# A macaron block on one core: the last two diagonal steps of causal attention in one PSUM bank, with another beginning of the first MLP and three other orders

## The chip, the core and the metric

The kernel runs on one core of a Trainium2 chip. The metric is the time on the device in microseconds (us), median of the runs shown. The core has five engines with a queue each, which run side by side: TensorE (PE, matrix products, with its weight loads shown apart as PEld), VectorE (DVE), ScalarE (ACT), GpSimd (POOL) and SyncE (SP, which here only issues DMAs). Each queue is worked off in order. PE writes to PSUM, which has 8 banks of 512 floats on each of the 128 partitions; everything else lies in SBUF.

## The reference

One block of 2048 tokens with 512 features: half an MLP, causal attention with 16 heads of 32, and half of the same MLP again, each behind a layer norm without weights. The MLP's weights are 4-bit codes with a scale for each 32.

```python
def _layernorm(x, axis=-1, eps=1e-05):
    m = jnp.mean(x, axis=axis, keepdims=True)
    v = jnp.var(x, axis=axis, keepdims=True)
    return (x - m) / jnp.sqrt(v + eps)
...
    qkv = jnp.einsum('bsd,ed->bse', x, w_qkv) + b_qkv
...
    scores = jnp.einsum('bhqd,bhkd->bhqk', q, k) / math.sqrt(Hd)
    causal = jnp.triu(jnp.full((S, S), -jnp.inf, dtype=scores.dtype), k=1)
    scores = scores + causal[None, None]
    attn = jax.nn.softmax(scores, axis=-1)
    out = jnp.einsum('bhqk,bhkd->bhqd', attn, v)
...
    gate = jnp.einsum('th,nh->tn', xt, Wg)
    up = jnp.einsum('th,nh->tn', xt, Wu)
    gelu = jnp.tanh(0.7978845608028654 * (gate + 0.044715 * gate ** 3)) * gate * 0.5 + gate * 0.5
    inter = gelu * up
    out = jnp.einsum('tn,hn->th', inter, Wd)
...
x = x + 0.5 * _L0_ffn_ref(_layernorm(x, axis=-1), ...)
x = x + _L0_attn_ref(_layernorm(x, axis=-1), ...)
x = x + 0.5 * _L0_ffn_ref(_layernorm(x, axis=-1), ...)
```

## The kernel before

Everything is computed in fp32 unless said otherwise. Each engine runs its instructions in the order in which the program issues them; that order is written out by hand in the loops below, and the waits between engines follow from which tile an instruction reads or writes and when a tile's buffer comes free.

**First MLP (`ffn`, L188).** The products are done with seven-product forms of 2 x 2 blocks (Strassen-Winograd). `slot` (L346) runs one unit of it: for the gate (m = 0) and then for the up weights (m = 1), the seven products in the order 1, 2, 6, 7, 5, 4, 3, each into one PSUM bank by `product` (L339, matmuls at L341), with the additions that turn them into four results spread over ACT, DVE and POOL behind each. After each product `pump(rate)` issues `rate` background steps (dequantisation of later weights), and then one group of `groups`, a list of other work such as normalisation. The beginning (L516 to L540) loads tokens and codes on SP's queue, normalises the first two token blocks with `Norm` (`n0`, `n1`; moments, scales, four `normal` and four `transposed` steps), dequantises the first gate and up weights (`gate`, `up`: six steps each half) and forms sums of transposed tokens (`token_sums`, L312) that products 3 to 7 need.

**Attention (`attention`, L1070).** Heads go in 8 pairs; a pair works on 4 blocks g of 512 queries. The keys go in chunks c of 128. Block g needs the chunks below it, 4g of them ("whole" ones), and four on the diagonal, c = 4g to 4g + 3, whose scores have 512, 384, 256 and 128 columns. That is 40 steps a pair: 4, 8, 12, 16. `STARTS` (0, 4, 12, 24) are the steps at which the blocks begin. `order(g)` puts the diagonal last, except in block 3, where half of the whole chunks come behind it.

A step (`step`, L1389) has for each of the two heads (a = 0, 1) the score matmuls into one PSUM bank (L1403 adds the negated row maxima as three rows in bf16, L1412 the scores), a mask on the diagonal (DVE L1428 for a = 0; for a = 1 an ACT copy L1432 and a POOL select L1433), the exponentials on ACT (L1439, L1441), and then in `tail` the sums of two steps' exponentials for the denominators (`sum`, POOL and DVE, L1461 and L1463) and, two steps later (`pending`), the `values` (L1332): matmuls at L1323 with the values, and for the sums with ones, into the one accumulator bank `av` (`ps_acc`, one buffer). `denominators` pops one pair's sum in every second step and at the end of a block. The two last diagonal steps are not summed; their exponentials go to the ones matmuls directly.

After the last step of a block ACT copies the accumulator to `both` (L1345; the pool `an` has two buffers of it), and for pairs 1 to 6 the denominators are turned over DMAs and inverted (`inverse`, four steps later). `divided` (POOL L1377) multiplies numerators with inverses, four pieces a block, at the steps that `when` names: 10, 10, 11 and 11 steps later for block 3, which is in the next pair.

Pairs 0 and 7 (`DOUBLE`) run two steps at a time (`attend(p, 2)`): both score sections, then both `rest`, then both `tail`. Their sums are split between DVE (a = 0) and POOL (a = 1), and their division is done at once in `chunk` (reciprocals on DVE L1366, products on POOL L1369).

In pairs 1 to 6 each step runs together with a step of `maxima(p + 1)` (L1231): scores of a query chunk against up to 512 keys (L1248), whose row maxima DVE takes (L1260, or L1256 with the mask on the diagonal). At a block's end `finish` reduces them (`nmax`, L1266), and POOL splits them into three bf16 pieces (`split`, L1271 and L1274), five small operations; `rows` transposes them three steps later (PE L1284, ACT L1288). `maxima(0)` and `maxima(1)` run together in a loop ahead (the front loop, L1528), with `take` pieces of the projections after each step. In the other pairs projection work fills the diagonal steps (`after_step`, L1493): `fill` holds a block's pieces and the number of diagonal steps left, 4 at the start.

**Orders touched.** In pair 7 the normalisation for the second MLP (`Norm("f2", ...)`) is put behind steps of block 3 by the two tuples `after`. In the second MLP (`second_ffn`, `pair`, L724) the four down sums of a piece are put at places 2, 5, 2 and 2 of a pair's work.

Of the kernel before, what the change touches and what calls it, by code (L numbers as in the profile page):

```python
# [19 lines left out]
P = 128  # L20
# [10 lines left out]
STARTS = (0, 4, 12, 24)  # L31
# [5 lines left out]
def macaron_kernel(ctx: ExitStack, tc: tile.TileContext, x, packed, scales, wqk, bqk, wv, bv, wo, bo, out):  # L37
# [150 lines left out]
    def ffn(phase, finish, behind, loads, ready=(), first_w=None):  # L188
# [8 lines left out]
        with tc.tile_pool(name=f"w{phase}", bufs=1) as wp, tc.tile_pool(name=f"dq{phase}", bufs=1) as dq, tc.tile_pool(  # L197
# [148 lines left out]
            def slot(g, rows, tp, sums, fill, rate, groups=()):  # L346


                groups = list(groups)
                b = token_factors(tp)  # L350
                inter = [
                    ap.tile(
                        [P, 2, 512], F32, tag=f"i{rows.h}_{tb}" if rows.h == 0 else f"i1_{tb % 2}",
                        name=f"inter_{phase}_{g}_{rows.h}_{tb}",
                    )
                    for tb in (2 * tp, 2 * tp + 1)
                ]
                gate = {}

                def gelu(cell, c):  # L360
                    nc.scalar.activation(c, c, AF.Gelu_apprx_tanh)
                    gate[cell] = c

                def gated(cell, c):
                    tt(inter[cell % 10 - 1][:, cell // 10 - 1, :], gate[cell], c, ALU.mult)

                for m, done in ((0, gelu), (1, gated)):
                    a = rows.factors(m)
                    nm = f"{phase}_{g}_{rows.h}_{tp}"
                    names = ("pg", "pu")  # L370

                    def temp(k, bufs=2):
                        return ap.tile([P, 512], F32, tag=k, name=f"{k}_{m}_{nm}", bufs=bufs)

                    for i in ORDER:
                        ps = ps_one.tile([P, 512], F32, tag="one", name=f"{names[m]}{i}_{nm}")
                        product(ps, a[i], b[i])
                        if i == 1:
                            u2 = temp("u2")
                            nc.scalar.copy(u2, ps)  # L380
                        elif i == 2:
                            c11 = temp("c11")
                            tt(c11, ps, u2, ALU.add)
                            done(11, c11)
                        elif i == 6:
                            tt(u2, ps, u2, ALU.add)
                        elif i == 7:
                            u3 = temp("u3")
                            tt(u3, ps, u2, ALU.add)
                        elif i == 5:  # L390
                            u4 = temp("u4")
                            nc.scalar.copy(u4, ps)  # L392
                            c22 = temp("c22")
                            tt(c22, ps, u3, ALU.add)
                            nc.gpsimd.tensor_tensor(u4, u4, u2, ALU.add)  # L395
                            done(22, c22)
                        elif i == 4:
                            tt(u3, ps, u3, ALU.add)
                            done(21, u3)
                        else:  # L400
                            tt(u4, ps, u4, ALU.add)
                            done(12, u4)
                        pump(rate)
                        if groups:
                            run(groups.pop(0))
                        if sums:
                            sums.pop(0)()
                        if fill:
                            fill.pop(0)()
                return inter  # L410
# [105 lines left out]
            if phase == 1:  # L516
                load_x(1)
                rows.load(0)
# [4 lines left out]
                tags = ["u3", "u3", "c11", "c11"]  # L523
                n0 = Norm("f1", 0, xT[0], normed)
                n1 = Norm(
                    "f1", 1, xT[1], lambda nm: ap.tile([P, D], F32, tag=tags.pop(), name=nm, bufs=2),
                    on_act=(), on_pool=(0, 1),
                )
                gate, up = rows.steps(0), rows.steps(1)
                tiles = n0.tiles()  # L530
                run(n0.moments + [n0.scales] + n1.moments + tiles[:6] + gate[:2] + [n1.scales] + tiles[6:])
                run([n1.normal[i] for i in (0, 2, 1, 3)] + [n1.transposed[i] for i in (2, 0, 3, 1)] + gate[2:])
                run(token_sums(0) + up)
# [10 lines left out]
            early = [[]]  # L544
            for n in (n2, n3):
                early += [[n.moments[0]], [], [n.moments[1]], [], [n.scales]]
            late = staggered(n2, n3) + [[s] for s in token_sums(1)]
            fill = ([], [])
            for g in range(NG):
                if g == 0:  # L550
                    first = [slot(g, rows, 0, *fill, 2, early)]
# [94 lines left out]
    def second_ffn(finish, ready, slots):  # L646
# [9 lines left out]
        with tc.tile_pool(name="w2", bufs=1) as wp, tc.tile_pool(name="act2", bufs=1) as ap:  # L656
# [371 lines left out]
            for n in range(2 * NP + 1):  # L1028
# [21 lines left out]
                if pieces:  # L1050
                    for k, f in enumerate(down_sums):
                        if due == (1, 1, 2, 3)[k]:
                            mine[(2, 5, 2, 2)[k]].append(f)
# [16 lines left out]
    def attention(xT, xT_f, wqk_wv, next_w):  # L1070
        with tc.tile_pool(name="aw", bufs=1) as aw, tc.tile_pool(name="qk", bufs=1) as qkp, tc.tile_pool(
# [159 lines left out]
            def maxima(p):  # L1231
# [5 lines left out]
                for g in range(NB):  # L1237
                    parts = an.tile([P, 2, 4, g + 1], F32, tag=f"parts{g}", name=f"parts_{p}_{g}")
                    whole = [(i, kb) for i in range(4) for kb in range(g)]
                    steps = around(g, whole, [(i, g) for i in (3, 2, 1, 0)])  # L1240
                    for i, kb in steps:
                        n = 512 if kb < g else (i + 1) * P
                        ps = [None, None]

                        def matmuls(a):
                            r = quadrant(p, a)
                            ps[a] = ps_one.tile([P, 512], F32, tag="one", name=f"pm_{p}_{g}_{i}_{kb}_{a}")
                            nc.tensor.matmul(  # L1248
                                ps[a][:, :n], lhsT=q[r, bass.ts(4 * g + i, P)], rhs=k[r, kb * 512 : kb * 512 + n],
                                start=True, stop=True,  # L1250
                            )

                        def rest(a, now):
                            most, scores = parts[:, a, i, kb : kb + 1], ps[a][:, :n]
                            if kb == g:
                                nc.vector.tensor_tensor_reduce(  # L1256
                                    scores, scores, mask_f[:, 512 - n :], 1.0, MASKED, ALU.add, ALU.max, accum_out=most
                                )
                            else:
                                nc.vector.tensor_reduce(most, scores, AX.X, ALU.max)  # L1260
# [36 lines left out]
            def attend(p, width):  # L1297

# [4 lines left out]
                def order(g):  # L1305
                    return around(g, list(range(4 * g)), list(range(4 * g, 4 * g + 4)))

                def columns(product, operand, off, **kw):


                    for a in range(2):
                        for h in range(2):
# [4 lines left out]
                            elif off <= (2 + h) * P:  # L1317
                                dst_ = avs[0][group, product, P:]
                                rhs = operand[:, a, (2 + h) * P : (3 + h) * P]
# [10 lines left out]
                def denominators():  # L1330
                    for operand, off in summed.pop(0):
                        columns(1, operand, off)  # L1332

                def values(g, n, off, pt):
                    c = order(g)[n]
# [3 lines left out]
                    columns(0, pt, off, v=vals[:, c, p % 4, :], start=(n == 0))  # L1339
                    last = n + 1 == len(order(g))  # L1340
                    if (n > 0 and n % 2 == 0) or last:
                        denominators()
# [46 lines left out]
                def step(g, n, copied):  # L1389
                    c = order(g)[n]  # L1390
                    off = max(0, c - 4 * g) * P
                    ps = [None, None]
# [6 lines left out]
                    def maxrows(a):  # L1399
# [3 lines left out]
                        nc.tensor.matmul(  # L1403
                            ps[a][:, off:],
                            lhsT=ones_b[r.start : r.start + 3, :],
                            rhs=m[r.start : r.start + 3, at_ * 512 + off : (at_ + 1) * 512],
                            start=True, stop=False,
                        )

                    def matmuls(a):  # L1410
                        r = rows_of(a)
                        nc.tensor.matmul(  # L1412
                            ps[a][:, off:],
                            lhsT=k[r, bass.ts(c, P)],
                            rhs=q[r, g * 512 + off : (g + 1) * 512],
                            start=False, stop=True,
                        )

                    def rest():
                        pt = pp.tile([P, 2, 512], F32, tag="pt", name=f"pt_{p}_{g}_{c}")  # L1420
                        scale = 1.0 / math.sqrt(HD)
                        plain = [off, off]
                        if c >= 4 * g:


                            for a in range(2 if p in DOUBLE else 1):
                                own = ps[a][:, off : off + P]
                                nc.vector.tensor_tensor(own, own, mask_k, ALU.add)  # L1428
                            if p not in DOUBLE:
                                plain[1] = off + P  # L1430
                                own = pt[:, 1, off : off + P]
                                nc.scalar.copy(own, ps[1][:, off : off + P])  # L1432
                                nc.gpsimd.affine_select(  # L1433
                                    out=own, in_=own, compare_op=ALU.is_ge, fill=MASKED, base=0,
                                    pattern=[[1, P]], channel_multiplier=-1,
                                )
                        for a in range(2):
                            if plain[a] < 512:
                                nc.scalar.activation(pt[:, a, plain[a] :], ps[a][:, plain[a] :], AF.Exp, scale=scale)  # L1439
                        if plain[1] > off:  # L1440
                            nc.scalar.activation(own, own, AF.Exp, scale=scale)  # L1441
                        two.append((pt, off))
# [296 lines left out]
```

## Time and profile before

| | |
|---|---|
| median of 3 runs | 3132.38 us (3132.2 to 3133.98) |
| profiled execution, its own time | 3135.08 us |
| its span | 3133.2 us |
| PE busy in the span | 3096.3 us |
| pairs 1 to 6, 1370 to 1950 us | PE busy 577.60 of 580, POOL 344.05, DVE 352.96, ACT 298.86 |
| pair 7 and the way to the second MLP, 1950 to 2041 us | PE busy 88.56 of 91, granted clock 0.96 |
| first 20 us | PE busy 7.71 |
| 20 to 70 us | PE busy 46.56 of 50 |

The span runs from the first to the last recorded instruction of the profiled execution; 1.9 us of its time lie around the span. Busy times are sums over an engine's instructions in a stretch. A timeline row gives the start, the time from the first start to the last end of a group of like instructions, the engine, the line, output and inputs by name and the number of instructions; in square brackets stands the time that the engine stood idle before, and what ended it. The granted clock is TensorE's, 1.00 being full speed.

### The profile page before, as it was taken

The page shows a single profiled execution, that of the slowest core. Times are in us where ns is not written, and L with a number is a line of the kernel's source. Part 1 is how long each engine was busy: PE and PEld are TensorE (multiplying, and loading weights), DVE is VectorE, ACT ScalarE, POOL GpSimd, SP SyncE. Part 2 cuts the span into 40 slices and gives each one's busy share as a digit, 9 for nine tenths or more (in the row PEclk, how much of TensorE's full clock was granted, in tenths as well). Part 3 has the DMA queues.
Part 4 walks back from the last instruction along what each step waited for, and adds up shares of the span by engine and source line. Part 5 has one row for each costly group of instructions (what it writes and reads, how often), then busy time and mean ns, then how long its engine had stood idle before and what let it go on. Part 6 is the DMA issues. An engine that isn't in the chain of part 4 may idle for free.

```text
span 3133.2 us, 45074 instructions
## 1 busy us (share of the span) xinstructions
PE 3096.3 (99%) x16608; PEld 1995.8 (64%) x16608; DVE 2069.6 (66%) x3217; ACT 1043.0 (33%) x2029; POOL 1521.9 (49%) x1512
## 2 busy tenths in 40 slices
PE   7999999999999999999999999999999999999999
PEld 4556565656565565444335434478888888888887
DVE  7676666666666656755564566777666776666676
ACT  5111111111111123265553456443333343333332
POOL 3757575857667672365663466522232223223221
PEclk9999999999999999999999999999999999999999
DMA  4223122212122221000000000064444445344442
GB/s 141 85 83 118 69 93 88 98 61 97 61 98 79 80 93 34 5 11 9 12 9 7 29 21 11 14 193 131 125 135 128 128 130 168 116 125 128 127 128 61
DMA packets 260394, 260.66 MB, mean 83 GB/s; under 512 B 20720, under 2 KB 224592, under 8 KB 256080
## 3 DMA queue, kind: packets, MB, share of 16 engines
q1 hardware_dynamic: 260176, 257.80, 25.3%
q8 instruction: 131, 2.15, 0.3%
q14 instruction: 87, 0.71, 0.1%
HBM read 175.74 MB, written 79.89 MB: 82 GB/s over the span
## 4 chain that ended last, share of the span: by engine, by line
PE 94%; DVE 2%; ACT 1%; issue 1%; POOL 1%; DMA 0%; SPq 0%; POOLq 0%; ACTq 0%; DVEq 0%
PE po L440 12%; PE d_f L748 12%; PE pu L341 12%; PE pg L341 12%; PE av L1323 7%; PE pod_f L879 7%; PE pm L1248 6%; PE f_f L748 6%; PE pqk L1146 4%; PE pof_f L879 3%; PE e_f L748 3%; PE ps L1403 2%; PE pp L1201 2%; PE pv L1175 2%; PE ps L1412 2%; PE poe_f L879 1%
## 5 line engine op out<-in xcount | busy, mean ns | idle before, releaser
L1439 ACT ACTIVATE pt<-ps 128x512 f32<-128x512 f32 (+3 forms) x616 | 289.1, 531 | 189.8 <-PE ps L1412 113.3
L748 PE MATMUL d_f<-ys_f,ring 128*128 128x256 f32 x1216 | 319.6, 383 | 6.1 <-DVE o_f L781 5.8
L1260 DVE TENSOR_REDUCE parts<-pm 128x1 f32<-128x512 f32 x384 | 245.1, 685 | 111.7 <-PE pm L1248 111.5
L1463 POOL TENSOR_TENSOR sum<-pt,pt 128x512 f32<-128x512 f32 (+1 forms) x210 | 249.2, 1205 | 121.2 <-ACT pt L1439 99.1
L1248 PE MATMUL pm<-kT,qT 32*128 32x512 f32 (+3 forms) x1280 | 297.2, 576 | 0.3 <-ACT kT L1152 0.3
L1412 PE MATMUL ps<-qT,kT 32*128 32x512 f32 (+3 forms) x1200 | 261.2, 539 | 0.0
L748 PEld LDWEIGHTS d_f<-ys_f,ring 128*128 128x128 f32 x1216 | 226.7, 190 | 53.6 <-DVE o_f L781 21.5
L802 DVE TENSOR_TENSOR o_f<-o_f,o_f 128x1024 f32<-128x1024 f32 x128 | 203.6, 1601 | 62.6 <-ACT o_f L787 57.9
L440 PEld LDWEIGHTS po<-wd,inter 128*128 128x128 f32 x1024 | 194.4, 190 | 77.5 <-issue 56.0
L440 PE MATMUL po<-wd,inter 128*128 128x256 f32 x1024 | 241.1, 379 | 0.0
L341 PE MATMUL pg<-xT_f,w 128*128 128x512 f32 x512 | 239.2, 595 | 1.1 <-ACT u L380 1.1
L341 PE MATMUL pu<-xT_f,w 128*128 128x512 f32 x512 | 238.0, 592 | 0.0
L894 POOL TENSOR_TENSOR xq<-xq,d_f 128x512 f32<-128x512 f32 x48 | 63.7, 1328 | 311.3 <-DVE xq L888 230.7
L454 POOL TENSOR_TENSOR xq<-xq,d 128x512 f32<-128x512 f32 x124 | 161.5, 1313 | 92.4 <-DVE xq L448 56.0
L894 POOL TENSOR_TENSOR xq_second<-xq_second,d_f 128x512 f32<-128x512 f32 x45 | 60.6, 1347 | 280.5 <-DVE xq_second L888 213.3
L1323 PE MATMUL av<-pt,vals 128*32 128x256 f32 (+1 forms) x2432 | 190.8, 369 | 1.9 <-ACT both L1345 1.7
L440 PEld LDWEIGHTS po<-wd,s 128*128 128x128 f32 x768 | 145.5, 190 | 57.9 <-issue 39.9
L395 POOL TENSOR_TENSOR u<-u,u 128x512 f32<-128x512 f32 x64 | 81.9, 1279 | 205.9 <-ACT u L392 205.9
L440 PE MATMUL po<-wd,s 128*128 128x256 f32 x768 | 181.4, 379 | 0.0
L802 POOL TENSOR_TENSOR o_f<-o_f,o_f 128x1024 f32<-128x1024 f32 x44 | 119.0, 2704 | 124.2 <-ACT o_f L787 123.1
L341 PE MATMUL pg<-xsum,w 128*128 128x512 f32 x384 | 177.8, 592 | 0.0
L341 PE MATMUL pu<-xsum,w 128*128 128x512 f32 x384 | 177.7, 592 | 0.0
(231 smaller groups left out, 6358.7 us busy)
## 6 DMA issues: line engine op xcount, KB each, us to landing
wd_f<-kept SPq DMA_DIRECT2D x112, 256.0 KB
kept<-wd SPq DMA_DIRECT2D x8, 1792.0 KB
xq<-in_x SPq DMA_DIRECT2D x16, 256.0 KB
pk<-in_gate_codes SPq DMA_DIRECT2D x16, 256.0 KB
sc<-in_gate_scales SPq DMA_DIRECT2D x32, 128.0 KB
pk<-in_up_codes SPq DMA_DIRECT2D x16, 256.0 KB
sc<-in_up_scales SPq DMA_DIRECT2D x32, 128.0 KB
pk<-in_down_codes SPq DMA_DIRECT2D x16, 256.0 KB
```

What stands on the lines that cost most here:

```text
L341: nc.tensor.matmul(ps, lhsT=a[:, j, :], rhs=b[:, j, :], start=(j == 0), stop=(j == 1))
L440: nc.tensor.matmul(ps[:, j, :], lhsT=a[i][:, k, bass.ts(2 * q + j, P)], rhs=b[i][:, k, :], start=(k == 0), stop=(k == 1),)
L454: adder.tensor_tensor(dst, dst, other, ALU.add)
L748: nc.tensor.matmul(ps[:, k, :], lhsT=fa[k][y], rhs=fb[k][y], start=first and k == 0, stop=True, skip_group_check=True,)
L802: sums.append(lambda: eng.tensor_tensor(dst, dst, other, ALU.add))
L879: nc.tensor.matmul(ps[:, j, :], lhsT=a[:, k, bass.ts(2 * q + j, P)], rhs=wd[:, PLACE[i], k, :], start=new and j == k == 0, stop=True, skip ...
L1248: nc.tensor.matmul(ps[a][:, :n], lhsT=q[r, bass.ts(4 * g + i, P)], rhs=k[r, kb * 512 : kb * 512 + n], start=True, stop=True,)
L1260: nc.vector.tensor_reduce(most, scores, AX.X, ALU.max)
L1323: nc.tensor.matmul(dst_, lhsT=lhsT, rhs=rhs, start=kw.get("start", False), stop=True, skip_group_check=True)
L1412: nc.tensor.matmul(ps[a][:, off:], lhsT=k[r, bass.ts(c, P)], rhs=q[r, g * 512 + off : (g + 1) * 512], start=False, stop=True,)
L1439: nc.scalar.activation(pt[:, a, plain[a] :], ps[a][:, plain[a] :], AF.Exp, scale=scale)
L1463: eng.tensor_tensor(s[:, a, off_2:], one[:, a, off_2:], other[:, a, off_2:], ALU.add)
```

## The change

**Attention.** In pairs 1 to 6 the last two diagonal steps become one. Its scores stand in one PSUM bank: 256 columns of chunk 4g + 2 at 0, and 128 of chunk 4g + 3 at 256. A pair has 36 steps, so `STARTS` is (0, 3, 10, 21); pairs 0 and 7 keep (0, 4, 12, 24) as `STARTS_2`. The maxima do the same for query chunks 1 and 0 of a block's diagonal, so the front loop has 36 steps too, with another `take`. A block's fill is spread over 3 diagonal steps instead of 4 in pairs 1 to 6. `order(g)` now yields tuples of chunks, and `values`, `columns`, `maxrows` and `matmuls` loop over the parts of a step.

The rule for when a sum's denominators are issued has become general: each sum is kept with its block and step, and `denominators` issues those of an earlier step. The sum of two steps is made as soon as `two` holds two.

```diff
-STARTS = (0, 4, 12, 24)
+STARTS = (0, 3, 10, 21)
+STARTS_2 = (0, 4, 12, 24)
...
                 def order(g):
-                    return around(g, list(range(4 * g)), list(range(4 * g, 4 * g + 4)))
+                    last = [2, 3] if width == 2 else [(2, 3)]
+                    return around(g, [(c,) for c in range(4 * g)], [(4 * g, ), (4 * g + 1, )] + [
+                        tuple(4 * g + i for i in (t if width == 1 else (t,))) for t in last
+                    ])
...
-                def denominators():
-                    for operand, off in summed.pop(0):
-                        columns(1, operand, off)
+                def denominators(g, n, last):
+                    while summed and summed[0][0] == g and (summed[0][1] < n or last):
+                        for operand in summed.pop(0)[2]:
+                            columns(1, *operand)
...
                     last = n + 1 == len(order(g))
-                    if (n > 0 and n % 2 == 0) or last:
-                        denominators()
+                    denominators(g, n, last)
...
+                    parts = [(off, 0)] if len(cs) == 1 else [(2 * P, 2 * P), (3 * P, P)]
...
-                        two.append((pt, off))
-                        pending.append(lambda args=(g, n, off, pt): values(*args))
+                        if len(cs) == 1:
+                            two.append((pt, off))
+                        else:
+                            summed.append((g, n, [(pt, *part) for part in parts]))
+                        pending.append(lambda args=(g, n, parts, pt): values(*args))
...
-                        if n % 2 == 1:
+                        if len(two) == 2:
...
-                take = 3 if n < 3 else 4 if n == 39 else 1 if n in (10, 11, 22, 23, 32) else 2
+                take = 4 if n == 35 else 3 if n in (0, 1, 2, 9, 20, 29) else 2
...
-                        fill = [fills[STARTS.index(n)], 4]
+                        fill = [fills[starts.index(n)], 4 if p in DOUBLE else 3]
```

In the maxima, `parts_of` holds one part of a step, or two where the key block is the diagonal one and i is 1:

```diff
-                    steps = around(g, whole, [(i, g) for i in (3, 2, 1, 0)])
+                    steps = around(g, whole, [(i, g) for i in (3, 2, 1)])
...
+                        parts_of = [(i, 0, n)] + [(0, n, n + P)] * (kb == g and i == 1)
```

**The beginning of the first MLP.** The first gate codes are loaded ahead of the second four token tiles; the first gate half is dequantised before the first tiles are normalised; the second block's normalisation is done on ACT alone; the first slot runs products 1 and 2 of gate and up first, pumps nothing after its first five products and three steps after each of the others, and the transposes of the second block and the token sums come between its products. `slot` takes an `order` and a list as `rate` for that.

```diff
             if phase == 1:
+                rows.load(0)
                 load_x(1)
-                rows.load(0)
                 rows.load(1)
...
-                tags = ["u3", "u3", "c11", "c11"]
+                tags = ["u3", "u3", "u4", "u4"]
                 n0 = Norm("f1", 0, xT[0], normed)
-                n1 = Norm(
-                    "f1", 1, xT[1], lambda nm: ap.tile([P, D], F32, tag=tags.pop(), name=nm, bufs=2),
-                    on_act=(), on_pool=(0, 1),
-                )
+                n1 = Norm("f1", 1, xT[1], lambda nm: ap.tile([P, D], F32, tag=tags.pop(), name=nm, bufs=2))
...
-                run(n0.moments + [n0.scales] + n1.moments + tiles[:6] + gate[:2] + [n1.scales] + tiles[6:])
-                run([n1.normal[i] for i in (0, 2, 1, 3)] + [n1.transposed[i] for i in (2, 0, 3, 1)] + gate[2:])
-                run(token_sums(0) + up)
+                run(n0.moments + [n0.scales] + gate[:4] + tiles + gate[4:])
+                run(n1.moments + [n1.scales] + n1.normal + up)
+                sums_0 = token_sums(0)
...
-            early = [[]]
+            t = n1.transposed
+            early = [[t[0]], t[1:3], [t[3]] + sums_0, []]
...
+            first_order = [(m, i) for m in range(2) for i in ORDER[:2]] + [(m, i) for m in range(2) for i in ORDER[2:]]
...
-                    first = [slot(g, rows, 0, *fill, 2, early)]
+                    first = [slot(g, rows, 0, *fill, [0] * 5 + [3] * 9, early, first_order)]
```

**Two more orders.** Pair 7's normalisation is put behind other steps, and one down sum of the second MLP comes four places later in one pair.

```diff
-                            after = ((0, 1, 4, 5, 6, 6, 7, 8, 9, 10), (3, 9, 11, 11, 12, 12, 13, 13, 14, 15))[tb][i]
+                            after = ((0, 1, 4, 5, 8, 8, 9, 9, 10, 11), (3, 9, 11, 11, 12, 13, 13, 14, 14, 15))[tb][i]
...
-                            mine[(2, 5, 2, 2)[k]].append(f)
+                            mine[(2, 5, 6 if n == NP + 2 else 2, 2)[k]].append(f)
```

## The prediction

> **What bounds the kernel now.** I read the busy times first, then the chain of waits, then a table of stretches, to see where TensorE (PE) isn't full.
>
> ```profile
> PE 3096.3 (99%) x16608; PEld 1995.8 (64%) x16608; DVE 2069.6 (66%) x3217; ACT 1043.0 (33%) x2029; POOL 1521.9 (49%) x1512
> PE 94%; DVE 2%; ACT 1%; issue 1%; POOL 1%; DMA 0%; SPq 0%; POOLq 0%; ACTq 0%; DVEq 0%
> ...
> 1370.00:1950.00 580.00, 577.60 (x5916) 243.46 (x5914) 352.96 (x886) 298.86 (x722) 344.05 (x523) 1.00 0.05 13
> ```
>
> PE is the bound: 99% busy, 94% of the chain. In the third line (pairs 1 to 6 of the attention; after the stretch's length come busy PE, weight loads, DVE, ACT, POOL) PE rests 2.4 of 580 us. So a PE section removed is a gain, but a wait put in front of PE costs in full. POOL is only 344 busy, but its queue is in order, and the change reorders it.
>
> **Part 1: two diagonal steps in one.** A step is a section S of scores (PE L1403, L1412, L1248), perhaps a section F of projection pieces, and a section A of values (L1323). The PE timeline of pair 2, block 1, prices S by column count:
>
> ```profile
> 1479.05 0.33 PE L1403 MATMUL ps<-wo_bo,ones_b 3*128 3x384 bf16 x1
> ...
> 1479.97 0.64 PE L1323 MATMUL av<-pt,vals 128*32 128x256 f32 x8
> ...
> 1484.17 0.28 PE L1403 MATMUL ps<-wo_bo,ones_b 3*128 3x256 bf16 x1
> ...
> 1484.82 0.64 PE L1323 MATMUL av<-pt,vals 128*32 128x256 f32 x8
> ...
> 1485.83 0.22 PE L1403 MATMUL ps<-wo_bo,ones_b 3*128 3x128 bf16 x1
> ...
> 1486.27 0.64 PE L1323 MATMUL av<-pt,vals 128*32 128x128 f32 x8
> ```
>
> From S's first start to A's: 0.92 for 384 columns, 0.65 for 256, 0.44 for 128. The merged step has the columns of the last two, 384 in all: 0.65 + 0.44 - 0.92 = 0.17 saved (0.29 in pairs without fill, where the 256 section takes 0.77). The two A sections behind become one; a section's fixed part is what S leaves at no columns, 0.44 - 0.25 = 0.19, and of it I count 0.14. So 0.31 in each of 16 blocks of pairs 2 to 5, 0.43 in 8 of pairs 1 and 6: **-8.4**. Fill: one piece takes 1.06, two in a section 1.92, so two one-piece sections joined save 0.20, in 12 blocks of pairs 3 to 5: **-2.4**. Front (maxima of pairs 0 and 1): 0.65 + 0.43 - 0.85 = 0.23 and 0.20 of fill in 4 blocks: **-1.7**. Together -12.5. All of it is PE time; ACT's and POOL's fewer instructions lie beside it.
>
> **What it puts in front of PE.** In the built order POOL now has, in the merged step, the five small operations that split the maxima AHEAD of the diagonal sum (L1461, L1463), and sum_2_1 ahead of the last two `divided` of the block 3 before. `both` has two buffers: the ACT copy of block 1 waits for those last two, and the next block's values wait for the copy, since the accumulator has one bank. Rows of before, same place, POOL, then ACT and PE:
>
> ```profile
> 1485.70 0.40 POOL L1461 COPY sum<-pt 128x256 f32<-128x256 f32 x1
> 1486.07 1.96 POOL L1463 TENSOR_TENSOR sum<-pt,pt 128x384 f32<-128x384 f32 x2
> 1488.10 1.52 POOL L1377 TENSOR_TENSOR attnT<-both,den 32x256 f32<-32x256 f32 x2
> 1489.70 0.29 POOL L1433 TENSOR_SCALAR_AFFINE_SELECT pt<-pt 128x128 f32<-128x128 f32 x1
> 1489.94 0.22 POOL L1271 CAST split<-nmax 128x8 bf16<-128x8 f32 x1
> ...
> 1491.39 1.52 POOL L1377 TENSOR_TENSOR attnT<-both,den 32x256 f32<-32x256 f32 x2
> 1492.99 2.50 POOL L1463 TENSOR_TENSOR sum<-pt,pt 128x512 f32<-128x512 f32 x2
> ```
> ```profile
> 1492.94 0.59 ACT L1345 COPY both<-av 128x512 f32<-128x512 f32 x1 [0.66 <-POOL attnT L1377]
> ```
> ```profile
> 1493.58 0.64 PE L1323 MATMUL av<-pt,vals 128*32 128x256 f32 x8 [0.62 <-ACT both L1345]
> ```
>
> The wait exists already: the copy starts as the last `attnT` ends, and PE stands still for 0.62. Now the new order, from the start of the merged scores at 0. DVE starts at 0.95 (as in the 384 step: 1479.05 to 1480.00), four maxima of 0.34 and 0.21 and two masks of 0.24 end at 2.5, nmax at 2.9. POOL: splits 1.4 to 4.3; sum 0.37 + 1.95 to 6.7 (its first half 5.7); `divided` 1.52 to 8.3; sum_2_1 2.50 to 10.8; `divided` 1.52 to 12.35; ACT copy 0.59; PE resumes at 13.0. PE by itself comes there at 0.92 + 1.00 + 1.18 + 0.57 + 1.19 + 1.43 + 0.34 + 1.26 = 7.9, and the fill of the merged step (pairs 2 to 6: 0, 1.06, 3.63, 1.06, 0). Stalls 5.1, 4.1, 2.5 (pair 4: the sum waits for exponentials until 9.4 there), 4.1, 5.1 = 20.9; pair 2 and pair 6 pay 1.2 and 1.3 already: **+18.4**. Bounds +6 (POOL 2.5 earlier) and +22.
>
> The sum itself: PE wants it in the merged step's A, near 5.5, and the second half is there at 6.7. Stall 1.1 in pairs without fill there: three blocks of pair 1, blocks 0 and 2 of pairs 2 and 6 (block 1 lies in the stall above, block 3 has no splits, fill covers the rest): 7 x 1.1 = **+7.7**, bounds 0 and 11.
>
> A pause can cost more than itself. Around 2002 PE paused three times (0.51, 0.66, 0.28), and the granted clock was 0.83, 0.50, 0.50, 0.50 in the next four stretches of 2 us: some 3 us lost. Pauses of 1.1, 0.8 and 1.5 at 46, 51 and 57 left it at 1.00. For five pauses of 2.5 to 5 us I take one such loss, **+3**, between 0 and 15.
>
> [...]
>
> **Part 2: denominators of pairs 0 and 7.** These run two steps at once; the rule `summed[0][1] < n` now asks for a double step's sum in the very next A, one double earlier.
>
> ```profile
> 1344.34 2.33 POOL L1369 TENSOR_TENSOR attnT<-both,den 32x128 f32<-32x128 f32 x4
> ...
> 1346.76 1.27 POOL L1463 TENSOR_TENSOR sum<-pt,pt 128x512 f32<-128x512 f32 x1
> ```
>
> That sum lies behind four chunk products and ends at 1348.03; A began at 1345.40, and after two value groups (0.45 each) and its first half PE would want it at 1346.4: 1.65 late. So by block: pair 0 about 0.7, 1.65, 1.6; pair 7 about 0.4, 1.75, 1.0: +7.1, bounds +3 and +11 (where ACT's exponentials end later). The last diagonal pair of block 3 is now added, 8 passes instead of 16: -0.4. **+6.7**.
>
> **Part 3: the beginning.** Gate codes come before x tile 1, so the first product starts near 15.05 instead of 19.64. But the up weights are ready at 20.8 only, and token sums come after the copies of tile 1, which stand behind ACT's normalisation and its first gelu: 28.3 by DVE's rows (1.44 + 1.63 behind 25.2), against 23.6. PE idles some 3 there, ten products of 1.72 follow, and the slot ends near 45.6 against 45.1. Later pauses of 3.4 shrink with 3 us less backlog on DVE; half of that, 1.7, against the 0.5 and a chance of the 3 us clock loss: I take **0**, bounds -4 and +4. SP's loads of x tiles 2 and 3 come later, not wanted before 30.
>
> **Part 4: three orders.** Pair 7's normalisation goes behind the next scores, around the pauses at 2002: -1, bounds -4 and +1. One down sum on DVE moves four places near 2574, where PE rests 3.4 of 20 us: 0, bounds -1 and +1. **-1**.
>
> **Sum:** -12.5 + 18.4 + 7.7 + 3 + 6.7 + 0 - 1 = **+22.3**. The profiled execution took 3135.08 (span 3133.2 and 1.9 around it), so 3157.4; the median shown is 2.7 below that execution: **3155 us**. The likeliest case's own range is 3143 to 3165.
>
> **Rivals.** *Gains alone (faster).* One mechanism: POOL reaches the last `divided` before PE does. Place: block 1 of pairs 2 to 6, and with it the diagonal sums. It decides when POOL's chain from nmax is 5 us shorter than I add up. For it: the page calls POOL's spans rough, and POOL is 41% idle there. Against: the rows lie end to end, and before already waits at this place. The sums of pairs 0 and 7 go through the same queue, so 18.4, 7.7, 3 and 7.1 all fall away: -13.9, 3118 to 3119.
>
> *Only the boundary wait.* Sums and doubles hidden, since PE, once delayed, comes later to all of them: -12.5 + 18.4 - 1 = +4.9, 3137. For it: one stall absorbs the next; against: pair 1 has no boundary stall, and pairs 0 and 7 lie elsewhere.
>
> *All upper ends.* +22, +11, five clock losses 15, doubles +11, beginning +4, less 13.5: +49.5, 3182 at the most; 3173 with three losses fewer. For it: 2002; against: 46 to 57.
>
> *The merge doesn't save.* If a PSUM bank written by two groups made S cost both sections (1.09), -8.4 falls to about -3: 3160, inside the main range.
>
> **Chances.** Forecast, with the unsaved merge: 0.52; boundary alone 0.15; gains alone 0.19; upper ends 0.14. About 0.2%, 6.3 us, can be told from no change: below 3126.1 faster, above 3138.7 slower. Of gains alone 0.17 is faster and 0.02 same (parts of it); of the boundary alone 0.10 is same, 0.05 slower. Faster 0.17, same 0.12, slower 0.71. The range leaves out about a tenth at each end: 3123 to 3168.
>
> **What would show it.** After: S of the merged step 0.92; in block 1 of pairs 2 to 6 `both` on ACT with an idle time ended by POOL attnT of 2 to 5 us, and PE av idle behind it; PE av on POOL sum in the diagonal blocks and in pairs 0 and 7; the stretch of pairs 1 to 6 about 15 us longer; the first pg near 15 and a PE gap ended by token sums near 28. A `both` that doesn't wait, or a shorter stretch, makes it wrong.

## The result and the profile after

The changed kernel takes 3172.56 us (median of 4 runs, 3169.96 to 3174.82) against 3133.06 before (the three runs known and one more): ratio 1.0124, 95% interval 1.0111 to 1.0136. It is slower by 39.5 us, some 17 more than forecast, and 4.6 beyond the top of the range. The profiled execution took 3169.96 us with a span of 3167.9 (before: 3135.08 and 3133.2). Each later ratio is to runs of before made beside that run, whose medians go from 3133.06 to 3134.63 us, so what two kernels differ by can come out 1 to 2 us apart by ratios and by times. Only runs in the chip's fast state count; two of the eight with three buffers (4840 and 5301 us) and one of before beside them (18198 us) were in a slow one.

Two lines of the page (busy times, and the chain of work that ended last), and the stretch of pairs 1 to 6 in the table of stretches (its length, busy PE, weight loads, DVE, ACT, POOL, the granted clock):

```profile
PE 3107.0 (98%) x16592; PEld 2008.7 (63%) x16592; DVE 2076.0 (66%) x3218; ACT 1038.0 (33%) x1961; POOL 1516.0 (48%) x1488
PE 91%; POOL 3%; DVE 3%; ACT 1%; issue 1%; DMA 1%; SPq 0%; DVEq 0%; POOLq 0%; ACTq 0%
...
1370.00:1990.00 620.00, 595.66 (x5988) 259.28 (x5984) 361.87 (x892) 293.86 (x656) 341.36 (x500) 0.98 0.05 12
```

PE now rests 24 us in that stretch instead of 2.4, POOL and DVE have 3% each of the chain, and over the whole kernel PE's busy time went up, from 3096.3 to 3107.0, though 16 matmuls left it: the clock is 0.98 in that stretch, so the same work takes longer. Idle time and slow time are two losses, and only the first stands in a table of waits.

Where the 34.7 us of span came from can be read off ACT's copies of `both`, one at each block's end, in the two timelines. How much later (or earlier) than before a block ends after the change, in us, and what the prediction's terms gave for the same stretch:

| stretch | measured | predicted |
|---|---|---|
| to the start of the front loop (first score matmul at 1191.38, before 1196.35) | -5.0 | 0 |
| front loop, to the first copy | +1.1 | -1.7 |
| rest of pair 0 | +4.8 | +3.9 |
| pair 1 | +2.7 | +1.6 |
| pairs 2 to 6 | +31.1 | +16.7 |
| pair 7 | +1.9 | +1.7 |
| second MLP and end | -1.9 | 0 |

Most of the miss lies in pairs 2 to 6, where block 1 of each pair costs 4.4, 4.8, 3.2, 4.8 and 4.4. The small gain in the second MLP isn't explained by a run; before lost 1.7 us of clock there, at 2589 to 2592, and after none past 2063. The same place as in the prediction, pair 2, in the timelines of POOL, ACT and PE; the merged scores start at 1489.23:

```profile
1492.83 0.22 POOL L1278 CAST split<-nmax 128x8 bf16<-128x8 f32 x1 [1.48 <-DVE nmax L1273]
...
1494.10 0.40 POOL L1488 COPY sum<-pt 128x256 f32<-128x256 f32 x1
1494.46 1.95 POOL L1490 TENSOR_TENSOR sum<-pt,pt 128x384 f32<-128x384 f32 x2
1496.49 1.51 POOL L1388 TENSOR_TENSOR attnT<-both,den 32x256 f32<-32x256 f32 x2
1498.08 2.48 POOL L1490 TENSOR_TENSOR sum<-pt,pt 128x512 f32<-128x512 f32 x2
1500.64 2.30 POOL L1388 TENSOR_TENSOR attnT<-both,den 32x256 f32<-32x256 f32 x3
```
```profile
1502.19 0.59 ACT L1356 COPY both<-av 128x512 f32<-128x512 f32 x1 [4.66 <-POOL attnT L1388]
```
```profile
1502.83 1.07 PE L1333 MATMUL av<-pt,vals 128*32 128x256 f32 x8 [3.77 <-ACT both L1356]
```

The order is the predicted one: splits, sum, two products, the next block's sum, the last products, and only then the copy. It comes 13.0 us after the merged scores and PE 13.6 (predicted 12.35 and 13.0). The matmul behind it shows what was under-priced: 1.07 for a group that takes 0.64. The granted clock there, and behind the same wait in pair 3 (busy PE, then the clock):

```profile
1502.00:1504.00 2.00, 1.18 (x12) 0.72 0.03 9
1504.00:1506.00 2.00, 2.00 (x10) 0.50 0.02 3
1506.00:1508.00 2.00, 2.00 (x24) 0.92 0.00 0
```
```profile
1606.00:1608.00 2.00, 1.87 (x14) 0.50 0.01 2
1608.00:1610.00 2.00, 2.00 (x16) 0.50 0.01 2
1610.00:1612.00 2.00, 2.00 (x18) 0.50 0.00 0
```

Summing (1 - clock) over stretches of 2 us gives the time lost: behind the five waits 1.72, 3.42, 1.72, 1.70 and 3.40, together 12.0 us. Before, the whole attention lost 3.4, all of it near 2006; after, it lost 13.7, with one more fall near 2060, in pair 7.

### The profile page after: what moved, and what is told of

Its sections match the earlier page's. It is cut to its first block, busy times and chain, and to the rows that moved or that the text cites. A ratio compares the mean times of both kernels' runs of the same rounds, so it can differ in the third digit from the quotient of the medians.

```text
span 3167.9 us, 44959 instructions
## 1 busy us (share of the span) xinstructions
PE 3107.0 (98%) x16592; PEld 2008.7 (63%) x16592; DVE 2076.0 (66%) x3218; ACT 1038.0 (33%) x1961; POOL 1516.0 (48%) x1488
## 4 chain that ended last, share of the span: by engine, by line
PE 91%; POOL 3%; DVE 3%; ACT 1%; issue 1%; DMA 1%; SPq 0%; DVEq 0%; POOLq 0%; ACTq 0%
PE po L441 12%; PE pg L343 12%; PE pu L343 12%; PE d_f L749 12%; PE pod_f L880 7%; PE av L1333 6%; PE f_f L749 6%; PE pm L1253 5%; PE pqk L1148 4%; PE pof_f L880 3%; PE e_f L749 3%; PE ps L1418 2%; PE pv L1177 2%; PE pp L1203 2%; PE ps L1428 2%; POOL sum L1490 2%
## 5 line engine op out<-in xcount | busy, mean ns | idle before, releaser
L1462 ACT ACTIVATE pt<-ps 128x512 f32<-128x512 f32 (+2 forms) x592 | 286.5, 546 | 239.2 <-PE ps L1428 128.7
L1333 PE MATMUL av<-pt,vals 128*32 128x256 f32 (+1 forms) x2432 | 181.5, 373 | 19.2 <-ACT both L1356 19.0
L1333 PEld LDWEIGHTS av<-pt,vals 128*32 128x32 f32 x2432 | 56.2, 109 | 199.7 <-issue 153.8
```

What stands on the lines that cost most here:

```text
L1333: nc.tensor.matmul(dst_, lhsT=lhsT, rhs=rhs, start=kw.get("start", False), stop=True, skip_group_check=True)
L1462: nc.scalar.activation(pt[:, a, x:y], ps[a][:, x:y], AF.Exp, scale=scale)
```

## The experiments

**Three buffers of `both`.** The wait is taken away by a buffer, so nothing of the order changes. (The other tiles of this tag, those of `normed`, get the third buffer in a second line of the edit.)

```diff
-                        both = an.tile([P, 2, 256], F32, tag="both", name=f"both_{p}_{g}")
+                        both = an.tile([P, 2, 256], F32, tag="both", name=f"both_{p}_{g}", bufs=3)
```

> The changed kernel with three buffers of `both` instead of two, nothing else. My theory: in block 1 of pairs 2 to 6 ACT's copy no longer waits for the last `divided` on POOL, so the five waits (about 18 us net of what the sums cost there anyway) go, and with them the five stretches of half clock behind them (10 us lost in the profiled run of after, 3.4 before). Expected 3172.6 - 18 - 11 = about 3143 us, clock lost under 5 us. Rival A: the low clock comes from the many short waits of PE, not from these five long ones: about 3155, clock lost still near 10. Rival B: the copy only stands in front of another wait of the same length (the accumulator, the sum): over 3165.

Measured 3144.82 us, ratio 1.0029 (1.0018 to 1.0041). The changed kernel had 1.0124, so 0.0095, or 30 us (28 by the medians), hung on this one buffer. What PE waited for in the attention, after and in this run (us in total, times, longest):

```profile
PE av L1333 <- ACT both L1356: 19.0, 8, 3.8
PE av L1333 <- POOL sum L1490: 10.0, 25, 0.8
```
```profile
PE av L1333 <- POOL sum L1490: 9.8, 24, 0.8
PE av L1333 <- ACT both L1356: 1.5, 3, 0.5
```

The long waits are gone and the second line is untouched. In pairs 1 to 7 no stretch is under 0.9 of the clock, and the line of the table that had 0.98 after now has 1.00:

```profile
1370.00:1990.00 620.00, 611.96 (x6296) 268.01 (x6292) 376.17 (x920) 309.80 (x691) 362.80 (x530) 1.00 0.05 13
```

Over the attention 5.1 us of clock are lost instead of 13.7, all of it ahead of pair 1, at 1209 to 1216 and 1318 to 1322. Both rivals fall: the low clock came from the five long waits, and no wait of their length took their place.

**The products one step earlier.** The same wait, taken away by the order, with two buffers.

```diff
-                            when = (..., (10, 10, 11, 11))[g]
+                            when = (..., (9, 9, 10, 10))[g]
```

> The changed kernel with the four `divided` of block 3 one step earlier, so that all of them stand ahead of sum_2_1 on POOL, with two buffers of `both` as in after. My theory: it is this place in POOL's queue that makes the long waits: the copy comes some 2.5 us earlier in each of five blocks, waits of PE there fall under 2 us, and the half clock behind them goes: 12 + 10 us less than after, about 3150. Rival: POOL's chain is too long whatever its order, the sum takes the place of the product: 3165 or more, half clock still there.

Measured 3148.94 us, ratio 1.0046 (1.0031 to 1.0061): 24 us less than after. PE waits 6.0 us for the copy, at most 1.2 at a time, and pairs 1 to 6 have no stretch under 0.9. The place in POOL's queue is the cause; POOL's chain is not too long for what must be done first.

**The sum ahead of the splits.** In the merged step the waiting sums are issued before the second half of the maxima, whose `finish` issues the splits. (`steps[0][3]` is the loop over `summing` with which `tail` began, now a function of its own.)

```diff
                     for _, _, rest, *_ in steps:
                         rest()
                     if other:
+                        steps[0][3]()
                         other[1](1, now)
```

> The changed kernel with the diagonal sum issued on POOL ahead of the maxima's splits in the merged step. My theory: the A section of the merged step took 2.98 instead of 1.43 us since the sum stood behind the splits; with the sum first about 16 us of such waits outside the boundary blocks go, and POOL reaches the last `divided` some 1.6 us earlier in each of five boundary blocks, 8 us. Expected about 3149 us, merged A sections under 1.6, the five long waits still there at about 4 us and still followed by half clock. Rival: the sum is late because of ACT's exponentials or the select, not the splits: no more than 5 us gained, 3168 or more.

Measured 3152.74 us, ratio 1.0054 (1.0036 to 1.0072): 22 us less than after by the ratios, 20 by the medians; 24 were expected. PE's wait for the POOL sum falls from 10.0 us in 25 times to

```profile
PE av L1333 <- ACT both L1356: 17.6, 8, 3.9
PE av L1333 <- POOL sum L1493: 3.7, 7, 0.8
```

while the long waits stay, and 13.7 us of clock are lost as in after. So the late sums and the long waits are two causes.

How a late sum costs more than its wait is seen in pair 1, block 2 of the changed kernel, where nothing else waits. PE's values of the merged step:

```profile
1425.90 0.65 PE L1333 MATMUL av<-pt,vals 128*32 128x128 f32 x12
1426.93 0.63 PE L1333 MATMUL av<-sum,ones_f 128*32 128x256 f32 x4 [0.39 <-POOL sum L1490]
1427.88 0.41 PE L1333 MATMUL av<-sum,ones_f 128*32 128x256 f32 x2 [0.32 <-POOL sum L1490]
...
1428.12 0.39 PE L1333 MATMUL av<-sum,ones_f 128*32 128x256 f32 x2
```

The profile counts 0.71 us of waiting, but the section takes 2.97 instead of the 1.43 that the same work takes elsewhere. The eight sum passes elsewhere run side by side in 0.61 (pair 2, block 1, at 1490.71); here the second head's half of the sum comes later, so they run as four, two and two, one group behind another. (Of POOL's two halves the first belongs to a = 0, the second to a = 1.)

**The old rule in pairs 0 and 7.**

```diff
-                        if len(two) == 2:
+                        if len(two) == 2 and (width == 1 or n % 2 == 1):
```

> The changed kernel with the old rule for pairs 0 and 7 (a double step's sum is made and registered at its second tail, so its denominators come one double step later). My theory: the pulled-forward denominators wait for POOL's half of the sum behind the chunk products; taking that back gives 5 to 10 us: about 3165. Rival: these pairs lose elsewhere (PE pauses from the beginning or from the norms), no change: 3172.

Measured 3157.93 us, ratio 1.0073 (1.0057 to 1.0089): 15 us less than after by the medians (16 by the ratios), 10 by the two profiled executions. In these pair 0 costs nothing any more (5.8 us less) and pair 7 is 5.9 us shorter, together 11.7; the five falls of the clock in pairs 2 to 6 took 3.4 us more in this execution than in after's. All of these are more than the prediction's 6.7. The place that the prediction showed, in the changed kernel, POOL and then PE:

```profile
1341.66 2.36 POOL L1380 TENSOR_TENSOR attnT<-both,den 32x128 f32<-32x128 f32 x4
1344.10 1.27 POOL L1490 TENSOR_TENSOR sum<-pt,pt 128x512 f32<-128x512 f32 x1
```
```profile
1344.27 0.60 PE L1333 MATMUL av<-sum,ones_f 128*32 128x256 f32 x4
1345.43 0.62 PE L1333 MATMUL av<-sum,ones_f 128*32 128x256 f32 x4 [0.56 <-POOL sum L1490]
```

The chunk products hold POOL until 1344.0, the sum ends at 1345.37, and PE issues the second head's four passes right then: a section of 2.60 instead of 1.43. Besides such places (five, 1.2 to 1.5 each) more than half of the other double steps with a sum lost 0.1 to 1.0, which I hadn't counted.

**The beginning alone**, on the kernel before: the diff's hunks of the first MLP and nothing else.

> The kernel before with the new beginning of the first MLP alone. In the trace of after the front loop of the attention begins 4.97 us earlier than before. My theory: all of it is from the beginning and stays: 3133.1 - 5 = 3128 us. Rival, the prediction's own: the early start is given back within the first MLP: 3131 to 3135.

Measured 3128.15 us, ratio 0.9981 (0.9972 to 0.9991): 6 us faster. PE's first product and the wait for the token sums in the changed kernel:

```profile
14.75 3.62 PE L343 MATMUL pg<-xT_f,w 128*128 128x512 f32 x4 [0.68 <-ACT xT_f L159]
...
27.00 3.24 PE L343 MATMUL pg<-xsum,w 128*128 128x512 f32 x7 [1.59 <-DVE xsum L324]
```

The start is as predicted (15.05), the wait is not: 1.6 us until 27.0, not 3 until 28.3, and without a fall of the clock. The pauses at 46, 51 and 57 (3.4 us) are gone entirely.

**The two other orders alone**, on the kernel before.

> The kernel before with the two other orders alone (pair 7's normalisation behind other steps, one down sum of the second MLP four places later). My theory: 1 us faster, at most 4, from the pauses and the half clock around 2002 us. Rival: the pauses only move (after shows one behind 2056 us, with half clock again), no difference that can be told.

Measured 3130.98 us, ratio 0.9993 (0.9985 to 1.0002). The interval holds 1, so it can't be told from nothing.

**The three repairs together**: the third buffer, the sum first, the old rule.

> The changed kernel with the three repairs together: three buffers of `both`, the diagonal sum ahead of the splits, the old rule in pairs 0 and 7. My theory: the merge itself saves what the prediction summed (12.5 us), the beginning 5 to 6, the orders about 1, and nothing of the waits stays: 18 us under before, ratio 0.994, some 3115 to 3118 us. Rival: the merged step saves less than its sections say, since other waits come up in their place (PE idle in the attention still over 10 us more than before): 3124 to 3130, no better than the new beginning alone.

Measured 3115.48 us, ratio 0.9940 (0.9928 to 0.9953). It beats both kernels. PE is full through pairs 1 to 6, and POOL has the sum ahead of the splits:

```profile
1370.00:1938.00 568.00, 567.50 (x5888) 250.91 (x5878) 359.19 (x887) 289.96 (x648) 338.46 (x499) 1.00 0.05 13
```
```profile
1483.42 1.95 POOL L1493 TENSOR_TENSOR sum<-pt,pt 128x384 f32<-128x384 f32 x2
1485.32 0.21 POOL L1278 CAST split<-nmax 128x8 bf16<-128x8 f32 x1
```

The one stretch with a low clock left in the attention is in the front loop, behind a wait for DVE's maxima at 1210, which leads to the next run.

**The front loop.** Half of a normalisation's moments, 1.7 us of DVE, behind step 1 instead of step 2, on the repaired kernel.

```diff
-                for step in norms[:2]:
+                ready = {1: 3, 2: 1}.get(n, 2)
+                for step in norms[:ready]:
```

> The repaired kernel (e5_repaired) with one half of a normalisation's moments, 1.7 us of DVE work, one step earlier in the front loop (behind step 1 instead of step 2). My theory: the front's 1.7 us didn't come since the merged step's eight maxima end later on DVE and the moments behind them (1204.75 to 1208.7 in after) hold the first whole maxima, so PE waits 1.4 us and the clock falls at 1210; with half of them earlier the wait goes: 1.4 plus some 1 of clock, 3113 us against 3115.5, clock not under 0.9 anywhere in 1200 to 1220. Rival: the wait comes from the banks, not from DVE's moments: 3115 to 3116, wait still there.

Measured 3111.25 us, ratio 0.9927 (0.9914 to 0.9941): 4.2 us by the medians, the fastest of all. The wait and the clock behind it in the repaired kernel, and the same stretch with the moved moments:

```profile
1210.47 1.18 PE L1253 MATMUL pm<-kT,qT 32*128 32x512 f32 x2 [1.38 <-DVE parts L1267]
```
```profile
1210.00:1212.00 2.00, 1.52 (x3) 0.85 0.00 0
1212.00:1214.00 2.00, 2.00 (x3) 0.50 0.00 0
1214.00:1216.00 2.00, 2.00 (x16) 0.79 0.00 0
```
```profile
1210.00:1212.00 2.00, 2.00 (x16) 1.00 0.00 0
1212.00:1214.00 2.00, 2.00 (x16) 1.00 0.02 4
1214.00:1216.00 2.00, 2.00 (x5) 1.00 0.00 0
```

1.4 us of waiting and 1.7 of clock are gone, and the profiled attention loses nothing to the clock at all. The rest of the 4.2 is no more than the medians scatter. The runs of the two kernels don't overlap (3114.85 to 3116.49, and 3110.45 to 3111.58), though the intervals of their ratios do.

**The old orders** on the repaired kernel.

> The repaired kernel (e5_repaired) with the old orders of pair 7's normalisation and of the down sum. My theory from e6_orders (0.9993, interval across 1): the orders are worth 1 to 3 us, so 3117 to 3119, with PE's pauses and half clock back in the last block of pair 7, where e5_repaired has no stretch under 0.9. Rival: worth nothing here, 3115 to 3116.

Measured 3116.02 us, ratio 0.9944 (0.9932 to 0.9957), 0.5 us from the repaired kernel: the rival's value. The half clock that I expected back in pair 7 didn't come. What the orders are worth stays below what these runs can tell.

## Why the prediction was right and wrong

The sign and the mechanism were right: PE is the bound, the merged step saves most of what it should, and POOL's new order puts more in front of PE than that. The sizes were not.

- **The merge, -12.5.** Nearly held. The repaired kernel with the old orders (0.9944) and the beginning alone (0.9981) differ by the merge and the repairs: 0.0037, 11.6 us, with intervals of 0.001 on each side. By the traces the fastest kernel is 1.6 shorter than before in the front and 11.2 in pairs 1 to 6, of which some 2.5 are the waits that before had in pairs 2 and 6 and the third buffer took away: some 10 for the merge. A merged S took 1.03 instead of 0.92, and in the changed kernel the front's 1.7 was eaten by DVE: its eight maxima of the merged step end later, the moments behind them hold the next ones. That queue I had not followed.
- **The boundary wait, +18.4.** Held, with its place, order and releaser: PE's five waits come to 17.5 us and the late sums of the same blocks to 4.3, together 21.8 where the prediction had 20.9, before it took off what pairs 2 and 6 paid already.
- **The clock behind it, +3.** This is the step that failed: "For five pauses of 2.5 to 5 us I take one such loss". All five were followed by a fall, 12.0 us in the profiled run, and so were the five of the run with the sum first and of that with the old rule. I had bounded the term at 15 and then chosen by the rows at 46 to 57, pauses of 0.8 to 1.5, though the five are about three times as long. What the runs showed in its place is a loss of 1.7 or 3.4 behind every pause of this length.
- **The sum behind the splits, +7.7.** Too small: the sections outside the boundary blocks lost 13.1. Seven places at 1.1 were counted; six of them lost 1.55 (nmax ended 3.5 us after the merged scores instead of 2.9, and the passes no longer ran side by side), one 0.75, and pairs 3 and 5, counted at nothing for their fill, 0.64 to 0.9 a block.
- **Pairs 0 and 7, +6.7.** Place and cause held; 11.7 by these pairs' stretches in the traces, 15 by the medians. The difference to 6.7 lies mostly in the other double steps with a sum, 5.0 in all, which I took as hidden; the five places themselves lost 6.2.
- **The beginning, 0.** Wrong the other way: -4 to -5 by the start of the front loop in the traces, 6 by the medians of the beginning alone. The later products found nothing to wait for; of the 3.4 us of their pauses only half had been counted, and that half set against a clock loss that didn't come.
- **The orders, -1.** Can't be told.
- **From the profile to the median.** The forecast took 2.7 off for the median lying below before's profiled run. After, the median lies 2.6 above it: 5.3 us, by itself more than what lay beyond the range, so that the time fell outside the range at all is in part chance. The four runs differ with their mean clock (0.996 at 3169.96, 0.994 at 3174.82).

Of the rivals, the one of the upper ends came nearest (3173 with three losses fewer), though by another mixture: the beginning at its lower end, clock, sums and doubles high. "Gains alone" is what the repaired kernel shows once POOL's order is mended, 3115 against its 3118 to 3119, with the beginning's gain, which that rival had at nothing.

In ten of the eleven profiled executions there are 29 falls of the clock in the attention (the eleventh, of the fastest kernel, has none), and summed in stretches of 1 us each loses 1.70 to 1.71 or 3.41 to 3.42 us. The length of a pause alone doesn't tell whether a fall follows: in the front loop of the repaired kernel 1.38 us of waiting were followed by one, and in after, at the same place, 1.38 us weren't. In the attention of the eleven 9 of 21 pauses of 1.4 us were followed by a fall, 2 of 4 of 1.9 us, and all 16 of 2.6 to 3.9 us, the shortest of after's five, 2.67 in pair 4, among them. The two falls left, before's near 2006 and one in the run of the beginning alone near 2003, stand behind several pauses of 0.1 to 0.7. What decides between two pauses of the same length no run shows.

## What to carry to other kernels

When instructions are merged or moved, write down the new order of every queue that feeds the bound engine, and follow each wait through buffer counts too: one more buffer, or one earlier step, was worth 24 to 30 us here. Price a pause of PE as long as those measured here, 2.6 to 3.9 us, at its length plus one of the clock's portions, 1.7 or 3.4 us, which all 16 of them cost; at 1.4 us it came in 9 cases of 21. And look at a slower kernel's parts one by one: this one held a change worth 18 to 22 us behind three wrong places in queues.

## What the runs showed of the hardware

The clock's losses came in two portions, 1.70 to 1.71 and 3.41 to 3.42 us in all 29 falls in the attention, behind pauses. The runs of one kernel scatter with their mean clock: after, with six falls in the profiled attention, by 4.9 us over four runs; the fastest kernel, with none there, by 1.1 over five; before, with one, by 6.9 over fifteen, from 3130.66 at a mean clock of 1.000 to 3137.55 at 0.998. The sum passes of the two heads hid one another where their operands came together, and not where one came late: eight passes that take 0.61 side by side took 1.58 (1426.93 to 1428.51) when one head's operand came 1 us later, of which the table of waits showed 0.32.
